# Moving the remaining additions of the values' products from VectorE to ScalarE and GpSimd, and building the identity matrix per stage

## The chip, the cores and the metric

The kernel runs on one NeuronCore of one Trainium2 chip. The metric is the device time of one execution in microseconds, the median of several. Besides TensorE (PE; its weight loads are listed as PEld) the core has VectorE (DVE), ScalarE (ACT), GpSimd (POOL) and SyncE (SP), which here issues all DMAs. Each engine works through its own instructions strictly in the order in which the program lists them and waits for the others through semaphores.

## The reference

The reference is a chain of four layers on `x` (8 sequences of 112 tokens, 512 channels) with a context `ctx` (8 x 375 rows, 512 channels), all in float32. Layer 0 is a cross attention. Layers 1 and 2 are recurrent blocks (RWKV): a time mix, whose core is a scan over the tokens, and a channel mix of three 512 x 512 products. Layer 3 is a decoder block with two cross attentions of 16 heads of 128 and an MLP.

```python
# layers 1 and 2, the scan over the tokens
a = k_l[..., :, None] * v_l[..., None, :]
out = jnp.einsum('bhs,bhst->bht', r_l, faaaa * a + s)
s_new = a + w_l[..., None] * s
# layer 3, in each of its two cross attentions
kh = (kv_in @ wk + bk).reshape(b, t, H, K)
vh = (kv_in @ wv + bv).reshape(b, t, H, K)
```

The values `vh` depend on the context and the weights alone, not on `x`. So they can be computed at any time before layer 3.

## The kernel before

**What fills what.** While layers 1 and 2 run, a generator `values()` computes the values of both attentions of layer 3, and two groups of keys, as a filler for TensorE. `fill(n)` takes its next n pieces. Its work is cut into 51 units; a unit multiplies a 2 x 2 arrangement of blocks by Strassen's scheme in Winograd's form, with seven products in place of eight, and the results are combined by additions. A product is two float32 matmuls 128x128x512, which the profile lists as four MATMUL records of L839.

**Banks.** The products of a unit go to two PSUM banks (tags `mm0` and `mm1`), and they alternate strictly: k1 in the first, k5 of the unit before in the second, then k6, k9 (of the unit before), k7, k2, k8, and the next unit has the banks exchanged. Each product is read out right after it: k1, k6 and k7 by a copy on ACT into a tile of the tag `v` (L922), k8 by a copy on ACT (L939), k2 by a copy on ACT into a tile of the tag `k2` and an addition on POOL (L932 and L933), k5 and k9 by an addition on DVE that reads PSUM and SBUF (L864 and L868). Until a bank has been read out, the second product after it can't start.

```python
p = bank(u, f, f"k5_{u}")
product(p, block(at), s["k5"])
nc.vector.tensor_add(u3, p, u3)
store(u3, u, 1, 1)
```

Every result is then written to memory by a DMA on SP (`store`, L855, L856 and L859), from where layer 3 reads it. SP also loads the context's blocks for the filler (`cv`, L823) and the rows of the values for the scan (`vj`, L534).

**The scan stages.** The function `time_mix` handles the recurrence in 64 steps (4 groups of channels times 16). There the order on PE, DVE, ACT and POOL is that of the source (`tc.manual_schedule(engines=ORDERED)`). A step has on DVE a product `kv` (L641, from PSUM and SBUF into PSUM) and the scan itself (L645, into `st`, two buffers); on ACT the copies of the next step's values into PSUM (`led`, L542 and L543), which wait for this step's `kv`, because `vp` has one buffer; on POOL the product `rs` (L649); on SP the load `vj` for three steps later (`spread`). Two fills stand in nearly every step: one between `kv` and `led`, the other after `rs`.

```python
nc.vector.tensor_mul(flat(kv), flat(vp), flat(k[:, c]))
fill(1)
vp = led(c * HS + at + 1)
...
nc.gpsimd.tensor_mul(by_batch(rs), st[:, :, :L], by_batch(r[:, c, :]))
waiting.append((c, j, rs))
fill(int(at not in (6, 10)))
```

After every fourth step TensorE sums `rs` (L622), and beside the steps run pieces of the group norm of the channels before (L561 to L583; its reciprocals on DVE, L575). Outside `manual_schedule` a scheduler places the instructions.

**The identity.** `ident`, 128 x 128, is made by two instructions of POOL at the start and stays in SBUF for the whole program. TensorE's transposes in layers 0 and 3 read it, and one subtraction (L743) at the start of the layers 1 and 2.

Of the kernel before, what the change touches and what calls it, by code (L numbers as in the profile page):

```python
# [22 lines left out]
F32 = mybir.dt.float32  # L23
# [6 lines left out]
P = 128  # L30
B, L, C, S = 8, 112, 512, 375
# [53 lines left out]
def halves(ap, h):  # L85

    return ap[..., h * NH : (h + 1) * NH]


def turned(ap):  # L90

    return ap.rearrange("p (h q r) -> p q h r", h=HB, q=4)


def turned_rows(ap, q):

    return ap.rearrange("(h q r) n -> q h r n", h=HB, q=4)[q]
# [11 lines left out]
def tile_kernel(ctx: ExitStack, tc: tile.TileContext, d: dict, out: bass.AP):  # L109
    nc = tc.nc  # L110

    const = ctx.enter_context(tc.tile_pool(name="const", bufs=1))
# [11 lines left out]
    def weight(name, g=None):  # L124

        w = wpool.tile([P, NC, C], F32, tag="w", name=f"w_{name}_{g}")
        nc.sync.dma_start(w, d[name] if g is None else d[name][g])
        return w

    x = xpool.tile([P, NC, N], F32, name="x")  # L130

    ident = const.tile([P, P], F32, name="ident")
    make_identity(nc, ident)
    mean_c = const.tile([P, P], F32, name="mean_c")
    nc.vector.memset(mean_c, 1.0 / C)
    eps = const.tile([P, 1], F32, name="eps")
# [12 lines left out]
    def mm(ps, name):  # L149
        return ps.tile([P, 512], F32, tag="mm", name=name)  # L150
# [65 lines left out]
    def layer0():  # L216
# [3 lines left out]
        with (  # L220
# [2 lines left out]
            tc.tile_pool(name="a0p", bufs=2, space=PSUM) as ps,  # L223
            tc.tile_pool(name="a0s", bufs=2, space=PSUM) as ps2,
        ):
            w_q, w_k = weight("L0_xattn_w_q"), weight("L0_xattn_w_k")
            nc.sync.dma_start(x, d["xT"])
            cxs = {}
# [69 lines left out]
            z = keep.tile([P, NC, N], F32, name="z0")  # L298
# [8 lines left out]
            for b in range(B):  # L307
# [7 lines left out]
                for t in range(3):  # L315
                    p = mm(ps, f"ps_r0_{b}_{t}")[:CT, :]
# [410 lines left out]
    def rwkv_layers():  # L727
        with tc.tile_pool(name="rc", bufs=1) as one:
            ones_t = one.tile([P, P], F32, name="ones_t")
            mean_h = one.tile([P, P], F32, name="mean_h")  # L730
            less_mean_h = one.tile([P, P], F32, name="less_mean_h")
            center_h = less_mean_h, mean_h
            pick = one.tile([P, 4, 4 * HB], F32, name="pick")
            with tc.tile_pool(name="rs", bufs=1) as setup:
                heads = setup.tile([P, P + P + HS - 1], F32, name="heads")
                nc.sync.dma_start(heads, d["heads"])

                nc.vector.tensor_copy(ones_t.rearrange("p (q h r) -> p q h r", q=4, h=HB), turned(heads[:, :P]))
                same = setup.tile([P, P], F32, name="same")
                for q in range(4):  # L740
                    nc.sync.dma_start(same[32 * q : 32 * (q + 1)], turned_rows(d["heads"][:, :P], q))
                nc.scalar.mul(mean_h.rearrange("p (q h r) -> p q h r", q=4, h=HB), turned(same), 1.0 / HS)
                nc.vector.tensor_sub(less_mean_h, ident, mean_h)  # L743

                for r in range(4):
                    at = P + HS - 1 - 4 * r
                    nc.vector.tensor_copy(pick[:, r], heads[:, at : at + 16 * HB - 3 : 4])
            first = one.tile([P, 2, NC, B], F32, name="first")
            nc.sync.dma_start(first, d["first"])
            for n in (1, 2):  # L750
                rwkv(n, ones_t, center_h, pick, first)


    def values():
# [8 lines left out]
        pool, spill, ps = shared["pool"], shared["spill"], shared["ps"]  # L763
# [4 lines left out]
        def tile_of(name):  # L768
            return pool.tile([P, C], F32, tag="v", name=name, bufs=6)
# [55 lines left out]
        def block(at):  # L825
            m = at // 2
            if m + 4 not in tiles:
                load(m + 4)
            return [tiles[m][:, n : n + P] for n in (at % 2 * BLOCK, at % 2 * BLOCK + CT)]
# [11 lines left out]
        def shaped(y, f):  # L841
            return y if f == "wv" else y[:, : HG * CT].rearrange("p (o s) -> p o s", o=HG)

        def bank(u, f, name):
            return shaped(ps.tile([P, C], F32, tag=f"mm{u % 2}", name=f"ps_v{name}"), f)

        def store(y, u, o, j):
# [10 lines left out]
            else:  # L858
                nc.sync.dma_start(where[:, t], y)  # L859

        def last_two(u, f, u2, u3, s, at):
            p = bank(u, f, f"k5_{u}")
            product(p, block(at), s["k5"])
            nc.vector.tensor_add(u3, p, u3)  # L864
            store(u3, u, 1, 1)
            yield "k5"
            product(p, block(at + 2), s["k9"], start=False)
            nc.vector.tensor_add(u2, p, u2)  # L868
            store(u2, u, 0, 1)
            yield "k9"  # L870

# [25 lines left out]
        for u, (at, unit) in enumerate(units):  # L897
            f, i, groups = sets[at]
            if unit == 0 and at == 2:

                for _ in before:
                    yield
                s = weights(at)
                yield
            elif unit == 0 and at:
                s = new
            if unit == UNITS - 2 and at != 1:
                new = {}
                steps = relay(at + 1, s, new)
                ready = next(steps)  # L910
            elif unit == UNITS - 1 and at != 1:
                following = ready
            if unit % 3 == 0:
                for gr in groups:
                    for b in (2 * (unit // 3), 2 * (unit // 3) + 1):
                        size = [P, 3, C] if f == "wv" else [P, 3, HG, CT]
                        shared[f, i, gr, b] = spill.tile(size, F32, name=f"{f}s{i}_{gr}_{b}")
            first, base, kept = bank(u, f, f"k1_{u}"), u * BLOCKS, []
            for what, n in (("k1", 0), ("k6", 2), ("k7", 4)):
                product(first, block(base + n), s[what], start=not n)  # L920
                kept.append(shaped(tile_of(f"{what}_{u}"), f))
                nc.scalar.copy(kept[-1], first)  # L922
                after(what)
                yield
                if n < 4:
                    yield from late()
            p1, u2, u3 = kept
            p = bank(u + 1, f, f"k2_{u}")
            product(p, block(base + 5), s["k2"])

            y = shaped(pool.tile([P, C], F32, tag="k2", name=f"k2_{u}"), f)
            nc.scalar.copy(y, p)  # L932
            nc.gpsimd.tensor_add(p1, y, p1)  # L933
            store(p1, u, 0, 0)
            after("k2")
            yield
            product(first, block(base + 6), s["k8"], start=False)
            y = shaped(tile_of(f"k8_{u}"), f)
            nc.scalar.copy(y, first)  # L939
            store(y, u, 1, 0)  # L940
            after("k8")
            yield
            before = last_two(u, f, u2, u3, s, base + BLOCKS + 1)
        for _ in before:
            yield
# [101 lines left out]

        return put

    def attention(i, h_in, work, kv, ps, ps2, keep, mlp_norm):  # L1050
        nonlocal filler
        pre = "L3_xattn_"
        scale = 1.0 / math.sqrt(HD)
# [64 lines left out]
        p = mm(ps, f"ps_bv{i}")[:, :HEADS]  # L1118
# [23 lines left out]
        for gr in range(NG):  # L1142
# [6 lines left out]
            for b in range(B):  # L1149
                u = f"{i}_{gr}_{b}"  # L1150
# [56 lines left out]
            if not ends:  # L1207
                add = add_to_x(None if gr else f"{pre}bo{i}")
# [63 lines left out]
    def layer3():  # L1272
        with (
            tc.tile_pool(name="t3v", bufs=2) as shared["pool"],
            tc.tile_pool(name="t3k", bufs=2) as kv,
            tc.tile_pool(name="t3", bufs=1) as keep,
            tc.tile_pool(name="t3w", bufs=2) as work,
            tc.tile_pool(name="t3p", bufs=2, space=PSUM) as ps,
        ):
            h_in = keep.tile([P, NC, N], F32, name="h_in")  # L1280
            with tc.tile_pool(name="t3s", bufs=1, space=PSUM) as ps2:
                def mlp_norm(h, bank):
                    if not h:
                        room = keep.tile([P, 3, 2, NH], F32, tag="t_h", name="t_mlp")
                        shared["t_mlp"] = room
                        squares = halves(h_in, 1)
                    else:
                        squares = halves(keep.tile([P, NC, N], F32, tag="q", name="room_mlp"), 1)
                    pre = "L3_xattn_ln_mlp_"
                    room = [None, squares] if h else [squares, None]  # L1290
                    room = room, shared["t_mlp"]
                    layer_norm_half(
                        ps, work, halves(h_in, h), h, pre + "scale", pre + "offset", "ln_mlp", room, bank
                    )

                for i in (1, 2):
                    attention(i, h_in, work, kv, ps, ps2, keep, mlp_norm)
            mlp(h_in, work, ps, keep, shared["t_mlp"])

    shared["spill"] = ctx.enter_context(tc.tile_pool(name="spill", bufs=1, space=bass.MemoryType.DRAM))  # L1300
# [84 lines left out]
```

## Time and profile before

| | |
|---|---|
| median of 3 runs | 3063.15 us (3061.47 to 3063.49) |
| profiled execution, its own time | 3068.96 us |
| span of its instructions | 3067.1 us |
| PE busy in the span | 2936.8 us (96%) |
| DVE, ACT, POOL busy in the span | 1698.1, 834.5, 767.3 us |
| first and second scan stage | 399 to 661 us, 1074 to 1345 us after the span's start |

The profile is of one execution. A row of a group of instructions gives its source line, engine, operation, output and inputs, sizes and count, then busy time, the mean of one, and the idle time of the engine just before it with what ended it. A row of waits gives who waited for whom: total, times, longest. The end of a matmul is modelled, so a short wait of PE can be hidden inside a busy time.

### The profile page before, as it was taken

How to read it: one execution, taken by the hardware profiler on the slowest of the kernel's cores; microseconds unless marked ns; L12 is line 12 of the kernel's file. 1: busy time of each engine (PE TensorE's matmuls, PEld its weight loads, DVE VectorE, ACT ScalarE, POOL GpSimd, SP SyncE). 2: the span in 40 equal slices, each digit the busy share in tenths (PEclk: the TensorE clock that was granted, in tenths of full speed). 3: DMA queues.
4: the chain of work that ended last, by engine and by line, in shares of the span. 5: the costliest groups of instructions: out<-in, count | busy, mean ns of one | idle time of the engine just before them, and what ended most of it. 6: DMA issues, size and time to landing. Idle time of an engine off the chain costs nothing.

```text
span 3067.1 us, 29702 instructions
## 1 busy us (share of the span) xinstructions
PE 2936.8 (96%) x10130; PEld 1585.1 (52%) x10130; DVE 1698.1 (55%) x2556; ACT 834.5 (27%) x1730; POOL 767.3 (25%) x668
## 2 busy tenths in 40 slices
PE   8989999998999999989989999999999999999999
PEld 4734433333434433337446666656566665656544
DVE  1433279876133289865165555655756454645555
ACT  2122145442232144532132222212222121212311
POOL 2232246642232257542210202020001101010030
PEclk9989999999999999999989999999999999999999
DMA  7322288963112299854234353424333343423110
GB/s 253 131 76 71 74 237 250 272 185 110 66 54 70 79 267 266 259 151 146 71 99 147 112 158 102 151 84 142 108 100 115 119 146 100 146 92 101 48 55 24
DMA packets 192054, 401.59 MB, mean 131 GB/s; under 512 B 26856, under 2 KB 112392, under 8 KB 185120
## 3 DMA queue, kind: packets, MB, share of 16 engines
q1 hardware_dynamic: 191904, 399.70, 42.0%
q8 instruction: 81, 1.33, 0.2%
q14 instruction: 69, 0.57, 0.1%
HBM read 321.85 MB, written 77.91 MB: 130 GB/s over the span
## 4 chain that ended last, share of the span: by engine, by line
PE 49%; DVE 2%; ACT 1%; issue 0%; POOL 0%; ACTq 0%; DVEq 0%; POOLq 0%
PE av L1180 6%; PE sc L1167 5%; PE ps_k1k L983 5%; PE ps_k7k L983 5%; PE ps_k5k L983 5%; PE pt L1170 3%; PE ps_k6k L983 2%; PE ps_k7q L983 2%; PE ps_k5q L983 2%; PE ps_k1q L983 1%; PE ps_k5o L983 1%; PE ps_k7o L983 1%; PE ps_k5fc L983 1%; PE ps_k7fc L983 1%; PE ps_k1o L983 1%; PE ps_k6q L983 1%
## 5 line engine op out<-in xcount | busy, mean ns | idle before, releaser
L839 PE MATMUL ps_vk<-wv,cv 128*128 128x512 f32 x1336 | 619.2, 611 | 52.4 <-DVE k L864 15.6
L839 PEld LDWEIGHTS ps_vk<-wv,cv 128*128 128x128 f32 x1336 | 251.5, 194 | 401.1 <-issue 303.0
L210 ACT ACTIVATE prob<-sc,top 112x376 f32<-112x376 f32 (+1 forms) x264 | 151.8, 575 | 709.6 <-DVE top L207 588.3
L649 POOL TENSOR_TENSOR rs<-st,r 128x896 f32<-128x896 f32 x128 | 246.7, 1928 | 226.7 <-DVE st L645 189.9
L645 DVE TENSOR_TENSOR_SCAN st<-decay,kv 128x904 f32<-128x904 f32 x128 | 260.4, 2035 | 15.6 <-DMA cv<-blocks 3.4
L1167 PE MATMUL sc<-k,q 128*112 128x376 f32 x512 | 200.6, 484 | 1.0 <-ACT prob L210 0.8
L1180 PEld LDWEIGHTS av<-pts,v 125*128 125x128 f32 (+1 forms) x1536 | 183.2, 191 | 30.0 <-DVE pts L1176 15.1
L1180 PE MATMUL av<-pts,v 125*128 125x112 f32 (+1 forms) x1536 | 186.6, 275 | 1.0 <-DVE pts L1176 1.0
L1160 POOL COPY k<-over_k 128x4 f32<-128x4 f32 x64 | 15.8, 253 | 678.3 <-PE sc L1167 610.0
L983 PE MATMUL ps_k1k<-cx,w_L_xattn_wk 128*128 128x375 f32 x480 | 177.1, 481 | 2.3 <-ACT rstdk L1001 2.3
L207 DVE TENSOR_REDUCE top<-sc 112x1 f32<-112x376 f32 (+1 forms) x264 | 143.6, 545 | 29.3 <-PE sc L1167 14.7
L641 DVE TENSOR_TENSOR kv<-vp,k 128x904 f32<-128x904 f32 x128 | 140.9, 1101 | 32.0 <-ACT vp L543 26.1
L922 ACT COPY k<-ps_vk 128x512 f32<-128x512 f32 (+1 forms) x153 | 89.0, 582 | 170.8 <-PE ps_vk L839 161.3
L1170 PEld LDWEIGHTS pt<-ident,prob 112*125 112x125 f32 (+1 forms) x768 | 97.6, 175 | 61.5 <-DVE prob L212 36.0
L212 DVE TENSOR_SCALAR prob<-prob,total 112x376 f32<-112x376 f32 (+1 forms) x264 | 120.7, 460 | 7.1
L983 PEld LDWEIGHTS ps_k1k<-cx,w_L_xattn_wk 128*128 128x128 f32 x480 | 89.3, 191 | 60.1 <-issue 3.2
L1170 PE MATMUL pt<-ident,prob 112*125 112x112 f32 (+1 forms) x768 | 116.3, 273 | 2.9 <-DVE prob L212 2.8
L543 ACT COPY vp<-vj 128x896 f32<-128x896 f32 x124 | 112.8, 910 | 11.6 <-DMA vj<-rows 7.6
L1187 DVE TENSOR_TENSOR ctxt<-av,bv 128x448 f32<-128x448 f32 x64 | 40.0, 624 | 126.6 <-PE av L1180 126.6
L933 POOL TENSOR_TENSOR k<-k,k 128x512 f32<-128x512 f32 (+1 forms) x51 | 67.4, 1322 | 133.6 <-ACT k L932 110.2
L1167 PEld LDWEIGHTS sc<-k,q 128*112 128x112 f32 x512 | 78.8, 176 | 41.1 <-ACT prob L210 6.1
L983 PE MATMUL ps_k7k<-cs,wsk 128*128 128x375 f32 x240 | 88.5, 480 | 0.6 <-DVE k L1088 0.6
(372 smaller groups left out, 4719.6 us busy)
## 6 DMA issues: line engine op xcount, KB each, us to landing
vj<-rows SPq DMA_DIRECT2D x124, 448.0 KB
cv<-blocks SPq DMA_DIRECT2D x181, 251.5 KB
cs<-blocks SPq DMA_DIRECT2D x120, 375.0 KB
wvs<-k SPq DMA_DIRECT2D x128, 256.0 KB
v<-wvs SPq DMA_DIRECT2D x64, 512.0 KB
cx<-in_ctxT SPq DMA_DIRECT2D x38, 750.0 KB
v<-wvs SPq DMA_DIRECT2D x64, 252.0 KB
wvs<-k SPq DMA_DIRECT2D x64, 224.0 KB
```

Of the source, the lines that this page charges most:

```text
L207: nc.vector.tensor_reduce(top, scores, AX.X, ALU.max, negate=True)
L210: nc.scalar.activation(prob, scores, AF.Exp, bias=top, accum_out=total)
L212: nc.vector.tensor_scalar(prob, prob, total, None, ALU.mult)
L543: nc.scalar.copy(vp[:, :, 1:], by_batch(vjs.pop((c, j))))
L641: nc.vector.tensor_mul(flat(kv), flat(vp), flat(k[:, c]))
L645: nc.vector.tensor_tensor_scan(flat(st), flat(decay[:, c]), flat(kv), 0.0, ALU.mult, ALU.add)
L649: nc.gpsimd.tensor_mul(by_batch(rs), st[:, :, :L], by_batch(r[:, c, :]))
L839: nc.tensor.matmul(to, left, right, start=start and n == 0, stop=k == 1, skip_group_check=True)
L983: nc.tensor.matmul(to, lhsT, rhs, start=start and k == 0, stop=k == 1, skip_group_check=not start)
L1167: nc.tensor.matmul(sc, q[:, o, tok], kt[:, o, :], start=True, stop=True)
L1170: nc.tensor.transpose(pt[t][:nt, o, :], prob[:, t0 : t0 + nt], ident[:L, :L])
L1180: nc.tensor.matmul(av[:, o, :], v[:nt, t, o * HD : (o + 1) * HD], pts[:nt, t, o, :], start=t == 0, stop=t == 2,)
```

## The change

k5 and k9 are read out as k2 was: a copy by ACT into a tile of the tag `k2`, and an addition by POOL. The tag `k2` gets two buffers. The identity is no longer kept throughout: it is made again in the pools of layer 0, of the setup of layers 1 and 2, and of layer 3.

```diff
-    ident = const.tile([P, P], F32, name="ident")
-    make_identity(nc, ident)
+    def identity(pool, name):
+        ident = pool.tile([P, P], F32, name=f"ident_{name}")
+        make_identity(nc, ident)
+        return ident
...
+            ident = identity(keep, "a0")
...
-                nc.vector.tensor_sub(less_mean_h, ident, mean_h)
+                nc.vector.tensor_sub(less_mean_h, identity(setup, "rs"), mean_h)
...
+        def add(y, p, u, f, what):
+
+            z = shaped(pool.tile([P, C], F32, tag="k2", name=f"{what}_{u}", bufs=2), f)
+            nc.scalar.copy(z, p)
+            nc.gpsimd.tensor_add(y, z, y)
+
         def last_two(u, f, u2, u3, s, at):
             p = bank(u, f, f"k5_{u}")
             product(p, block(at), s["k5"])
-            nc.vector.tensor_add(u3, p, u3)
+            add(u3, p, u, f, "k5")
             store(u3, u, 1, 1)
             yield "k5"
             product(p, block(at + 2), s["k9"], start=False)
-            nc.vector.tensor_add(u2, p, u2)
+            add(u2, p, u, f, "k9")
             store(u2, u, 0, 1)
             yield "k9"
...
-
-            y = shaped(pool.tile([P, C], F32, tag="k2", name=f"k2_{u}"), f)
-            nc.scalar.copy(y, p)
-            nc.gpsimd.tensor_add(p1, y, p1)
+            add(p1, p, u, f, "k2")
             store(p1, u, 0, 0)
...
-    def attention(i, h_in, work, kv, ps, ps2, keep, mlp_norm):
+    def attention(i, ident, h_in, work, kv, ps, ps2, keep, mlp_norm):
...
+            ident = identity(keep, "l3")
```

## The prediction

> **What bounds the kernel now.** I start with the busy shares of the page. PE is at 9 in almost every slice, so time is won only where PE stands still.
>
> ```profile
> span 3067.1 us, 29702 instructions
> PE   8989999998999999989989999999999999999999
> DVE  1433279876133289865165555655756454645555
> ```
>
> DVE's 7 to 9 in slices 6 to 9 and 15 to 18 mark the two scan stages. The table by windows gives the sums for the first (399 to 661), the stretch between, and the second (1074 to 1345); the columns are length, PE, PEld, DVE, ACT, POOL.
>
> ```profile
> 399.00:661.00 262.00, 246.36 (x729) 98.74 (x730) 235.44 (x175) 126.49 (x235) 162.37 (x96) 0.97 0.86 254
> 661.00:1074.00 413.00, 394.99 (x951) 175.19 (x950) 146.50 (x164) 103.69 (x187) 113.62 (x125) 0.96 0.26 81
> 1074.00:1345.00 271.00, 252.60 (x747) 101.46 (x746) 235.80 (x177) 129.46 (x238) 163.37 (x97) 0.98 0.87 252
> ```
>
> PE and DVE are both near full there (94% and 90%), and in-order queues tie them together. Next, PE's waits over the whole program:
>
> ```profile
> PE ps_vk L839 <- DVE k L864: 15.6, 10, 5.8
> PE ps_vk L839 <- DVE k L868: 14.0, 9, 3.1
> ...
> PE ps_vk L839 <- ACT k L922: 6.8, 7, 2.4
> PE ps_vk L839 <- ACT k L939: 6.1, 5, 1.7
> ```
>
> The two longest are the additions that the change moves: 29.6 us in 19 waits, 9.8 in the first stage, 12.8 in the second, 7.0 elsewhere. The timeline shows one:
>
> ```profile
> 506.37 1.53 DVE L575 RECIPROCAL gsq<-gsq 128x224 f32<-128x224 f32 x1
> ...
> 507.82 1.08 DVE L641 TENSOR_TENSOR kv<-vp,k 128x904 f32<-128x904 f32 x1
> 508.81 0.68 DVE L864 TENSOR_TENSOR k<-ps_vk,k 128x512 f32<-128x512 f32 x1
> ...
> 509.54 1.13 PE L839 MATMUL ps_vk<-wv,cv 128*128 128x512 f32 x2 [2.22 <-DVE k L864]
> ```
>
> PE's product was done near 507.3; its addition stood in DVE's queue behind a reciprocal and the `kv` after it, and PE waited 2.22 us for the bank.
>
> **What the Trainium skill says.** "PSUM — Partial Sum Buffer" (The four PSUM rules): GpSimd can't touch PSUM; hence the copy by ACT. The trace agrees in so far as no POOL row reads a PSUM tile. "Perfetto Trace Analysis" (Matmuls): groups should rotate through banks so that one's evacuation overlaps the next one's matmuls. Here two banks alternate; the 2.22 us are that overlap failing. "SBUF — State Buffer" (Who interferes with whom): a DVE instruction with two SBUF inputs contends with GpSimd instructions that read SBUF. The trace agrees: in the scan stages, where `vp` and `kv` lie in PSUM, L933 takes 1260 to 1291 ns; beside L691 (two SBUF inputs) it took 2.51 and 2.37 us, and L691 itself 671 to 2759 ns.
>
> **The change part by part.**
>
> *DVE loses 102 additions* (2 for each of 51 units, median 0.68 us), 17 units in each stage: 34 x 0.68 = 23 us, to 212 us. What PE gets depends on where the fill stands. Ahead of the step's `led`, the copy by ACT needs only the product: in the first stage three waits (2.2, 1.4, 2.7) vanish, 6.4 us. After the scan, the DVE addition ended 2.03 + 0.68 = 2.71 us after `kv`; on ACT it stands behind `led`, 0.17 + 0.91 + 0.58 = 1.66 us after `kv`, so at most 1.05 us of each is gained. Capping the nine waits of this kind at 1.05 each, 6.7 us go; the two at a stage's first steps (2.2 and 3.1), where `led` is done long before, go whole, 5.3. Together 18.4 of 22.6. Of the 7.0 us elsewhere I take 6.5: the largest, 5.8 us at 760, is an addition behind DVE's L691 while ACT is idle. **Gain 25 us** (bounds 15 and 29.6).
>
> *ACT gets 102 copies* of 0.585 us: 34 x 0.585 = 20 us per stage, 146 of 262, not a bound. But its copies make PE wait too: 12.9 us for the 255 of L922, L932 and L939, 0.05 each; 102 more: **loss 5 us** (0 to 10). Queued behind them are `led`, and with it DVE's next `kv`.
>
> *POOL gets 102 additions* of 1.27 us (L933): 34 x 1.27 = 43 us per stage, 162 to 206. It fits the stage. Queued behind an addition, which now waits for ACT, is `rs`, and for `rs` wait the sums L622 (slack of two steps) and, by the two buffers of `st`, the scan two steps on: a slack of about 1.1 + 2.03 + 1.1 after a scan's end, less 1.93 of `rs`, 2.3 us. One addition fits; it doesn't where the relay of weights puts POOL additions of 2.6 us (L783's row) beside it, once per stage: **loss 2 us** (0 to 6). Outside the stages 34 additions can collide with DVE's two-input operations, each up to 1.2 us, mostly beside PE work: **loss 1 us** (0 to 8).
>
> *SP issues the same DMAs in the same number*, but the stores of k5 and k9 now wait for POOL. SP's waits in the first stage:
>
> ```profile
> SPq L859 <- POOL k L933: 38.2, 11, 5.3
> ...
> SPq L855 <- POOL k L933: 14.5, 5, 4.3
> SPq L859 <- DVE k L864: 9.7, 7, 2.7
> SPq L859 <- DVE k L868: 9.1, 8, 2.8
> SPq L855 <- DVE k L868: 8.1, 5, 1.8
> SPq L855 <- DVE k L864: 7.7, 5, 2.4
> ```
>
> A store behind POOL waits 52.7 / 16 = 3.3 us, one behind DVE 34.6 / 34 = 1.0. The 34 moved stores come 2.3 us later, and behind them stand `cv` loads (issued eight products ahead, so covered) and the next `vj`. From the DMA packets of the 124 `vj` loads I took when each had landed and when ACT's copy began: the slack has a median of 5.3 us, but 9 loads have under 1.2. The shortfall, the sum of (2.3 - slack) where positive, is 17 us; 34 of 64 steps have a moved store: 9 us. It delays ACT and DVE, which now have room, so I take about half: **loss 5 us** (0 to 19, the latter for a delay of 3.1).
>
> *The k2 buffers.* A copy waits for the addition two before it, four products or some 7 us earlier; nothing (up to 2 us of loss if POOL is late).
>
> *The identity*: two more pairs of a memset (0.20) and a select (0.29) on POOL. The one of the setup runs while POOL waits 57.9 us for weights (L780), and its reader L743 comes 20 us later; the one of layer 3 stands beside a wait of PE of 9.2 us (for the norm's mean), whose DVE sums run slow beside POOL's additions: between -1 and +1 us, I take 0. Freed and added SBUF move addresses; in the built program the loads at the filler's start wait for the same instructions as before: 0.
>
> Sum: 25 - 5 - 2 - 1 - 5 = **12 us faster**. On its own time the profiled execution would go from 3068.96 (span 3067.1 and 1.9 around it) to 3057. The median of the runs is 5.8 us below that execution, so the prediction is 3063.15 - 12 = **3051 us**.
>
> **The rivals.**
> 1. *The cover holds* and ACT's queue costs nothing: 25 to 29.6 us less POOL's 2, 3035 to 3040. For it: median slack of 5.3 us of `vj`, DVE 50 us below the stage. Against: ACT already makes PE wait 12.9 us.
> 2. *The wait only changes its owner*: ACT's copy stands behind `led`, which waits for `kv`, which waits for the reciprocal; PE waits as before. ACT gives a third of the gain or nothing: 25/3 less 8 is 0, so 3057 to 3067. For it: at 1257 PE waited 2.2 us for L864, and ACT's own copy then came only at 1258.79, after `led`. Against: in eleven of the 14 waits of the stages `led` was done before PE began to wait.
> 3. *Slower: SP's queue becomes the pacemaker.* Late stores make `vj` late, ACT waits with `led` and all copies behind it, PE for the banks. At 2.3 us of delay the unhalved price is 9 us, at 3.4 us it is 0.53 x 44 = 24, at 4.0 it is 0.53 x 65 = 35. It decides from about 3 us on, where it and the 8 of ACT and POOL eat the gain; at 4 us the time is 3063 - 25 + 8 + 35 = 3081. For it: POOL's additions stand behind a `rs` of 1.93 us, and single stores waited up to 5.3. Against: SP is often early (27.1 us of waits of `cv` loads for PE in the first stage), so part of the delay is idle time.
> 4. *POOL becomes the bound* by contended additions of 2.5 us: 162 - 17 x 1.27 + 51 x 2.5 = 268 us per stage, over the 262 of now, some 3080. It decides from 2.04 us each (245 us per stage). Against it: 1291 ns is the longest there. 2 in 100, counted with 3.
>
> That the change doesn't do what it says is excluded by the built program: DVE 102 fewer instructions, ACT 102 more, POOL 106 more, PE and SP as many as before and in nearly the same order.
>
> **How the numbers follow.** A measurement of this kernel can tell about 0.2%, 6 us, from no change. Forecast (3044 to 3057): 0.42. Rival 1: 0.25. Rival 2: 0.17. Rivals 3 and 4: 0.16. Faster is the first two, 0.67; same rival 2, 0.17; slower 0.16. The range goes from 3032, a little below rival 1 (0.07 left out), to 3069, where 0.13 of rival 3 is left out. The faster cases alone span 3032 to 3057.
>
> **What would show it.** Right: PE's waits for the bank of k5 and k9 name ACT and sum to under 12 us; both stages are shorter by 5 to 10 us each; L869's additions take 1.27 us in the stages; SP's waits for POOL grow to over 130 us per stage; waits of ACT's L543 copy for `vj` grow from 7.6 us by about 10. Wrong: these waits grow by over 30 us (rival 3), PE's waits for ACT reach 25 us (rival 2), or POOL's additions are much longer than 1.3 us in the stages (rival 4).

## The result and the profile after

| | before | after |
|---|---|---|
| median | 3063.49 us (5 runs, 3061.47 to 3071.53) | 3051.93 us (5 runs, 3042.98 to 3054.23) |
| ratio | | 0.994, 95% interval 0.9924 to 0.9956 |
| profiled execution | 3068.96 us | 3052.01 us |

By the medians of these runs the change makes the kernel 11.6 us (0.4%) faster, where 12 were forecast. The ratio, which is estimated from all runs, says 0.6%, 18 us (13 to 23); in a second series it was 0.9937 (0.9917 to 0.9957), 19 us. Compared at one clock of PE (explained below) the gain is 13.9 us. So the sum came out about right, but partly by luck: its gain was too small by 7 to 11 us and its price by 6 to 9, and these errors cancelled.

The page of the changed kernel, its head first and then three of its groups (busy time, mean of one, idle time before them and its cause):

```profile
span 3050.0 us, 29875 instructions
...
PE   8989999999999999999899999999899999999999
...
DVE  1533268866223287856265565655756564645555
...
L649 DVE TENSOR_TENSOR_SCAN st<-decay,kv 128x904 f32<-128x904 f32 x128 | 260.7, 2037 | 24.5 <-POOL rs L653 6.4
L869 POOL TENSOR_TENSOR k<-k,k 128x512 f32<-128x512 f32 (+1 forms) x153 | 201.1, 1315 | 239.3 <-ACT k L868 207.3
...
L547 ACT COPY vp<-vj 128x896 f32<-128x896 f32 x124 | 112.8, 910 | 22.7 <-DMA vj<-rows 18.9
```

Most lines have moved by a few; the copy is now L868 and the addition L869, for k2, k5 and k9 alike. DVE's scan (L649) has a new wait for POOL, 6.4 us, and ACT's copy of `vj` (L547) waits 18.9 us where in the kernel before it waited 7.6:

```profile
ACT vp L543 <- DMA vj<-rows: 7.6, 5, 2.5
```

The table by windows, for the first scan stage, the stretch between, and the second (length, then busy time of PE, PEld, DVE, ACT, POOL, then PE's clock):

```profile
405.00:661.00 256.00, 242.79 (x731) 98.74 (x732) 218.57 (x142) 145.14 (x269) 204.11 (x130) 0.99 0.89 260
661.00:1067.00 406.00, 392.08 (x946) 174.64 (x945) 142.97 (x147) 111.16 (x201) 138.54 (x141) 0.96 0.26 82
1067.00:1328.00 261.00, 249.01 (x749) 101.42 (x748) 218.73 (x142) 147.10 (x273) 205.45 (x131) 0.99 0.90 259
```

From its first `kv` to its last, the first stage is shorter by 6.9 us (263.1 to 256.2), the second by 11.1 (271.6 to 260.5), the stretch between by 5.7. Part of this is the clock. Intervals at half clock took 6.8 and 5.1 us of full clock from the two stages before, 3.4 and 1.7 here. In a second profile of the changed kernel (`a2_changed`), where they took 5.1 and 6.8, the stages are shorter by 5.4 and 5.6 us. POOL has 204 us of work in the first stage and is no bound. The stretch ahead of the first stage is 5.8 us longer here; the profiles below put that down to the clock for the most part.

PE's waits over the whole program (total, times, longest):

```profile
PE ps_vk L843 <- ACT k L932: 10.5, 9, 2.4
...
PE ps_vk L843 <- ACT k L868: 6.9, 5, 3.3
PE ps_gm L565 <- ACT gsq L566: 6.5, 6, 3.3
...
PE ps_vk L843 <- ACT k L946: 3.6, 3, 1.4
```

No bank waits for DVE any more. The four rows of before summed to 42.5 us; the three of now (L932, L868, L946) make 21.0.

### The profile page after: what moved, and what is told of

It reads as the page before. It is cut to its first block, busy times and chain, and to the rows that moved or that the text cites. A ratio compares the mean times of both kernels' runs of the same rounds, so it can differ in the third digit from the quotient of the medians.

```text
span 3050.0 us, 29875 instructions
## 1 busy us (share of the span) xinstructions
PE 2931.5 (96%) x10130; PEld 1585.6 (52%) x10130; DVE 1656.9 (54%) x2454; ACT 888.3 (29%) x1832; POOL 898.6 (29%) x774
## 4 chain that ended last, share of the span: by engine, by line
PE 82%; DVE 7%; POOL 4%; DMA 3%; issue 3%; ACT 2%; SPq 0%; DVEq 0%; POOLq 0%; ACTq 0%
PE ps_vk L843 12%; PE av L1187 6%; PE sc L1174 5%; PE ps_k1k L990 5%; PE ps_k7k L990 5%; PE ps_k5k L990 5%; PE ps_o L161 3%; PE pt L1177 3%; PE ps_k6k L990 2%; PE ps_r L472 2%; PE ps_k L472 2%; PE ps_v L472 2%; DVE st L649 2%; PE ps_k7q L990 2%; PE ps_fk L161 2%
## 5 line engine op out<-in xcount | busy, mean ns | idle before, releaser
L843 PE MATMUL ps_vk<-wv,cv 128*128 128x512 f32 x1336 | 606.4, 604 | 34.3 <-ACT k L932 10.5
L649 DVE TENSOR_TENSOR_SCAN st<-decay,kv 128x904 f32<-128x904 f32 x128 | 260.7, 2037 | 24.5 <-POOL rs L653 6.4
L869 POOL TENSOR_TENSOR k<-k,k 128x512 f32<-128x512 f32 (+1 forms) x153 | 201.1, 1315 | 239.3 <-ACT k L868 207.3
L1187 PEld LDWEIGHTS av<-pts,v 125*128 125x128 f32 (+1 forms) x1536 | 184.8, 193 | 29.7 <-DVE pts L1183 14.5
L1177 PEld LDWEIGHTS pt<-ident_l,prob 112*125 112x125 f32 (+1 forms) x768 | 97.4, 176 | 61.5 <-DVE prob L215 35.9
L868 ACT COPY k<-ps_vk 128x512 f32<-128x512 f32 (+1 forms) x153 | 89.1, 583 | 136.1 <-PE ps_vk L843 135.5
L932 ACT COPY k<-ps_vk 128x512 f32<-128x512 f32 (+1 forms) x153 | 89.0, 582 | 114.6 <-PE ps_vk L843 111.2
L547 ACT COPY vp<-vj 128x896 f32<-128x896 f32 x124 | 112.8, 910 | 22.7 <-DMA vj<-rows 18.9
L1177 PE MATMUL pt<-ident_l,prob 112*125 112x112 f32 (+1 forms) x768 | 116.1, 273 | 2.7 <-DVE prob L215 2.6
```

What stands on the lines that cost most here:

```text
L649: nc.vector.tensor_tensor_scan(flat(st), flat(decay[:, c]), flat(kv), 0.0, ALU.mult, ALU.add)
L843: nc.tensor.matmul(to, left, right, start=start and n == 0, stop=k == 1, skip_group_check=True)
L869: nc.gpsimd.tensor_add(y, z, y)
L1177: nc.tensor.transpose(pt[t][:nt, o, :], prob[:, t0 : t0 + nt], ident[:L, :L])
L1187: nc.tensor.matmul(av[:, o, :], v[:nt, t, o * HD : (o + 1) * HD], pts[:nt, t, o, :], start=t == 0, stop=t == 2,)
```

## The experiments

**How they are compared.** Runs of one kernel differ by up to 24 us, and they follow the mean clock that was granted to PE: a common slope fitted within the kernels through 143 timed runs is -2.05 us for each 0.001 of clock, and it leaves about 2 us of scatter (3.3 and 4.5 us for the runs of `e1_identity` and `e6_vj5`). So beside each measured ratio stands the mean time brought to a clock of 0.981; two such means differ reliably from some 3 us on, for `e6_vj5` from 4. Whether a kernel causes its clock isn't settled by this, so both columns are given. The rows come from three series, each with its own runs of the kernel before (medians 3064.0, 3070.0, 3066.7; at one clock 3063.8, 3064.9, 3063.1). The second holds `e4_k2_one`, `e5_st3`, `e6_vj5` and `e9_no_add_outside`, and no run of the changed kernel. Measured from the kernel before in their own series, these four would look 1.2 us better than below.

| run | median us | ratio to before (95%) | mean clock | us at 0.981 |
|---|---|---|---|---|
| before, all series | 3065.8 | 1 | 0.9801 | 3063.7 |
| changed, first runs | 3051.9 | 0.9940 (0.9924 to 0.9956) | 0.9816 | 3050.3 |
| `e1_identity` | 3063.4 | 0.9999 (0.9984 to 1.0013) | 0.9804 | 3062.5 |
| `e2_dve_copy` | 3078.2 | 1.0038 (1.0023 to 1.0054) | 0.9811 | 3077.3 |
| `e3_no_add` | 3023.8 | 0.9870 (0.9851 to 0.9889) | 0.9852 | 3033.0 |
| `e7_late_store` | 3043.9 | 0.9939 (0.9922 to 0.9955) | 0.9837 | 3050.7 |
| `e4_k2_one` | 3051.6 | 0.9938 (0.9918 to 0.9957) | 0.9823 | 3053.6 |
| `e5_st3` | 3043.7 | 0.9912 (0.9889 to 0.9935) | 0.9842 | 3049.3 |
| `e6_vj5` | 3039.9 | 0.9899 (0.9878 to 0.9920) | 0.9852 | 3047.5 |
| `e9_no_add_outside` | 3042.2 | 0.9906 (0.9885 to 0.9927) | 0.9834 | 3045.9 |
| `a2_changed` | 3045.3 | 0.9937 (0.9917 to 0.9957) | 0.9833 | 3049.4 |
| `e10_st3_vj4` | 3043.0 | 0.9933 (0.9914 to 0.9952) | 0.9825 | 3046.3 |
| `e11_all` | 3056.0 | 0.9972 (0.9961 to 0.9984) | 0.9798 | 3054.3 |
| `e12_no_add_inside` | 3035.1 | 0.9904 (0.9883 to 0.9924) | 0.9848 | 3042.0 |

At one clock the changed kernel (11 runs of two series, 3049.8) is 13.9 us faster than before.

### The identity alone (`e1_identity`)

Against the kernel before, `ident` is built by stages as in the diff, and k5 and k9 stay with DVE:

```diff
         def last_two(u, f, u2, u3, s, at):
...
-            add(u3, p, u, f, "k5")
+            nc.vector.tensor_add(u3, p, u3)
...
-            add(u2, p, u, f, "k9")
+            nc.vector.tensor_add(u2, p, u2)
```

(The minus lines are those of the changed kernel; `k2` has one buffer.)

> The identity by stages alone; k5 and k9 are still added by DVE. Forecast's term: 0, so 3063 us, ratio to the kernel before 1.000 (0.998 to 1.002). Rival: the 5.8 us by which the first scan stage of the changed kernel starts later (404.9 against 399.1 us) come from the identity or from moved addresses; then the stage starts at about 405 us here too, and the time is near 3069 us, ratio 1.002.

The ratio is 0.9999, so the identity and the moved addresses cost nothing that can be told. PE's waits (L874 and L878 are the additions by DVE here) are those of before:

```profile
PE ps_vk L843 <- DVE k L874: 16.3, 13, 5.8
PE ps_vk L843 <- DVE k L878: 14.6, 8, 3.1
```

The first stage began at 402.1 us in this profile, at 399.1 in that of before, and in the changed kernel at 404.9 in one profile and at 392.3 in the other. The clock's records explain most of this spread: in the changed kernel's two profiles the half-clock intervals ahead of the stage took away 25.6 and 10.2 us of full clock. One and the same kernel starts the stage 12.6 us apart, so the later start is not shown to be an effect of the edit.

### DVE copies, POOL adds (`e2_dve_copy`)

```diff
-            nc.scalar.copy(z, p)
+            (nc.scalar.copy if what == "k2" else nc.vector.tensor_copy)(z, p)
```

> As the changed kernel, but DVE copies k5 and k9 out of PSUM instead of ACT, so that DVE keeps as many instructions as before and only POOL's additions and SP's later stores are new. Forecast's sum: no gain of 25, no 5 of ACT, but the losses of POOL (2 + 1) and SP (5): 8 us slower than the kernel before, 3071 us, ratio 1.0026. Rival (POOL and SP cost nothing, all of the change is what PE waits for): 3063 us, ratio 1.000. Rival (SP's queue is the pacemaker): over 3080 us, ratio over 1.005.

The copy takes DVE 68.9 us in 102 times, as the additions of before did (69.0), so this run has all that the change adds on POOL and SP and nothing of what it takes from DVE. PE's waits (L868 is the copy of k5 and k9):

```profile
PE ps_vk L843 <- DVE k L868: 29.2, 19, 2.8
...
PE ps_vk L843 <- ACT k L932: 6.9, 7, 2.4
PE ps_vk L843 <- ACT k L946: 6.0, 5, 1.7
```

29.2 us in 19 waits is what before had (29.6 in 19). The run is 13.6 us slower than before at one clock (ratio 1.0038): this is the price of the new additions and stores while DVE copies, where 8 were forecast. And it is 27.5 us slower than the changed kernel, which differs from it in nothing but the engine of the copy: the move to ACT, its own stalls taken off, is worth 27.5 us, where the forecast had 25 - 5 = 20. The price need not be made of the same parts in both kernels: POOL's additions make DVE's operations 3.4 us longer in sum here (1774.7 us against 1771.3 before), 16.3 in the changed kernel (1718.6 against 1771.3 - 69.0). The rival with SP's queue as pacemaker (over 3080) falls.

### Without POOL's additions (`e3_no_add`)

```diff
         def add(y, p, u, f, what):
 
+            if what != "k2":
+                nc.scalar.copy(y, p)
+                return
             z = shaped(pool.tile([P, C], F32, tag="k2", name=f"{what}_{u}", bufs=2), f)
```

> As the changed kernel, but ACT's copy of k5 and k9 goes straight into the tile that is stored, and POOL's addition is left out (two of the four blocks of each value lack a term). DVE is as free as in the changed kernel, POOL as busy as before, and the stores wait for ACT alone. Forecast's sum: gain 25 less 5 of ACT, without the 8 of POOL and SP: 3043 us, ratio 0.9935. Rival (these losses are nothing): as the changed kernel, 3051 us, ratio 0.996. Rival (they are more than double): under 3035 us, ratio under 0.991.

The ratio of 0.987 is that of the rival: 16.8 us less than the changed kernel at one clock, so the new additions and what follows from them cost about twice the forecast's 8. The run also gives the gain without any price of POOL and SP: it is 30.7 us faster than the kernel before at one clock, where the forecast had 20.

### Where this price lies: outside and inside the stages (`e9_no_add_outside`, `e12_no_add_inside`)

A flag is set around the 64 steps of each scan stage. The first run leaves the additions of k5 and k9 out where it isn't set (17 units), the second, with `shared.get("scan")` without the `not`, where it is (34 units):

```diff
-            z = shaped(pool.tile([P, C], F32, tag="k2", name=f"{what}_{u}", bufs=2), f)
+            if what != "k2" and not shared.get("scan"):
+                nc.scalar.copy(y, p)
+                return
+            z = shaped(pool.tile([P, C], F32, tag="k2", name=f"{what}_{u}", bufs=2), f)
```

> As the changed kernel, but POOL's addition of k5 and k9 is left out in the 17 units outside the scan stages (there ACT copies into the tile that is stored; some blocks of the values lack a term). Theory (contention outside: in the changed kernel DVE's L694 group takes 131.4 us against 120.1 where all these additions are left out, and the partial sums of the norms 51.9 against 46.1): this alone gives about 10 us of the 17, 3040 us at the same clock, ratio near 0.992. Forecast's term (1 us): 3049 us, ratio 0.995. Rival (the cost lies in the stages): as the changed kernel, 3050 us.

Outside, it is 3.9 us at one clock, four times the forecast's 1, but not 10. (The 131.4 and 120.1 us of the expectation are sums over the operations of that kind in layers 1 and 2; the line named there, L695 here, has 44.3 and 34.0.) Here is what POOL's additions do to DVE's operations with two SBUF inputs. First the changed kernel's groups on DVE by line (busy time, mean ns), then the same in this run, where L695 has become L697:

```profile
L695 DVE SCALAR_TENSOR_TENSOR xk<-sxc,vecs,xc 128x448 f32<-128x448 f32 x16 | 25.5, 1642 | 6.6 <-POOL sxc L355 6.2
...
L179 DVE TENSOR_TENSOR part_mean_ln<-part_mean_ln,x 128x448 f32<-128x448 f32 x16 | 18.2, 1136 | 0.4
```

```profile
L697 DVE SCALAR_TENSOR_TENSOR xk<-sxc,vecs,xc 128x448 f32<-128x448 f32 x16 | 21.5, 1392 | 6.2 <-POOL sxc L355 5.7
...
L179 DVE TENSOR_TENSOR part_mean_ln<-part_mean_ln,x 128x448 f32<-128x448 f32 x16 | 14.4, 898 | 0.4
```

One `xk` takes 1642 ns on the mean in the changed kernel, where additions of k5 and k9 fall beside some of them, and 1392 without these additions (1367 in the kernel before). Over all of DVE this is 17.9 us of longer operations (1718.6 against 1700.7 us, summed over instructions). PE's waits show what comes through. The longest of them, first in the changed kernel, then in this run:

```profile
PE ps_t L422 <- DVE xx L412: 11.0, 14, 3.5
```

```profile
PE ps_t L422 <- DVE xx L412: 9.0, 12, 3.5
```

With `xk` (4.4 and 3.9) and the norms' partial sums (3.8 and 1.6), PE waits 19.2 us for such operations in the changed kernel and 14.5 here: 4.7 us less, near the 3.9. The rest of the 17.9 lies beside PE's work. That such operations get longer is what "SBUF — State Buffer" (Who interferes with whom) of the Trainium skill lets one expect, and the trace agrees.

> As the changed kernel, but POOL's addition of k5 and k9 is left out in the 34 units inside the scan stages (some blocks of the values lack a term); the complement of the run that left it out outside. If the two parts add up to the 17 us at the same clock of the run that left out all: 13 us faster than the changed kernel beside it. Forecast's terms for the stages (POOL 2, SP 5): 7 us faster. Rival (the cost of POOL and SP in the stages lies beside PE's work): under 3 us faster.

Inside, it is 7.8 us (10 us by the medians of the two kernels in this series), near the 7 that the forecast's POOL and SP terms made. But what these 7 consisted of was wrong, as the waits of ACT show in this run:

```profile
ACT vp L547 <- DMA vj<-rows: 17.0, 11, 3.3
ACT v L583 <- POOL v L581: 14.7, 16, 2.6
```

No store waits for these additions here, and ACT still waits 17.0 us for `vj` (20.4 in the changed kernel of the same series). What falls, beside the scan's wait for `rs` (6.4 to 0.9 us), is another wait: that of ACT's last step of the group norm (L583, before L579) for POOL's multiplication ahead of it (L581, before L577). In the changed kernel and in the kernel before it is

```profile
ACT v L583 <- POOL v L581: 22.1, 16, 4.8
```

```profile
ACT v L579 <- POOL v L577: 14.6, 13, 2.6
```

The multiplication stands behind POOL's new additions, and behind ACT's waiting instruction stand the copies that free the banks. That wait was in no term of the forecast. How many of the 7.8 us it carries was not tried alone.

PE's own waits show where the price inside arrives. PE's sums (L626) wait for `rs` 4.5 us in the changed kernel of the same series and 2.0 here:

```profile
PE ps_y L626 <- POOL rs L653: 4.5, 3, 2.2
```

```profile
PE ps_y L626 <- POOL rs L654: 2.0, 2, 1.0
```

For the group norm's square on ACT, PE waits 6.1 us there and 4.5 here, for ACT's releases of the banks 23.1 and 20.3. Together that is 33.7 against 26.8, 6.9 us (5.1 with the first profile of the changed kernel).

The two parts make 11.7 us, both together 16.8: with an uncertainty of 2 us or more, some 4 to 5 us remain unexplained.

### The terms inside the stages (`e7_late_store`, `e5_st3`, `e6_vj5`, `e10_st3_vj4`)

The store of k5 goes one piece later:

```diff
             add(u3, p, u, f, "k5")
-            store(u3, u, 1, 1)
             yield "k5"
             product(p, block(at + 2), s["k9"], start=False)
+            store(u3, u, 1, 1)
```

> As the changed kernel, but the store of k5 is issued one piece later, behind the product of k9, where POOL has added by then; in SP's queue a load of the filler and the next vj now come ahead of it. Forecast's term of SP (5 us, of which k5 has about half): SP's waits for POOL in the first stage fall from 107 to about 60 us, ACT's waits for vj from 18.9 to about 12 us, and the time by 2 to 3 us to 3049, ratio 0.995. Rival (late vj costs nothing, since kv of DVE waits beside PE's work): waits fall, the time stays at the changed kernel's.

SP's waits for POOL in the first stage, which in the changed kernel are

```profile
SPq L863 <- POOL k L869: 68.8, 33, 5.2
SPq L859 <- POOL k L869: 38.2, 15, 4.9
```

fell only to 100 us (62.9 + 37.2, over 396 to 657), those of ACT for `vj` in both stages not at all (18.9 and 18.8), and at one clock the time is that of the changed kernel (+0.9 us). The edit moved less than was meant, so it is a weak test of SP's term.

A third buffer for `st`, in the tile of the first two `vj` (`early`), which is free after the second step:

```diff
-                        st = work.tile([P, B, LP], F32, tag="st", name=f"st{n}_{c}_{j}", bufs=2)
+                        if (c * HS + at) % 3 == 2:
+                            st = early[:, : B * LP].rearrange("p (b l) -> p b l", b=B)
+                        else:
+                            st = work.tile([P, B, LP], F32, tag="st", name=f"st{n}_{c}_{j}", bufs=2)
```

> As the changed kernel, with three buffers of st (the third lies in the unused part of the tile that holds the first vj). DVE's waits of the scan for rs, 6.3 us in 3 times, should go. Forecast's term of POOL: 2 us, so 3048 us. Theory after the first runs (POOL and SP cost 13 to 17 us at the same clock, most of it contention of POOL's additions with DVE outside the scan stages): at most 4 us faster than the changed kernel, ratio 0.994 to 0.995. Rival (most of the cost comes through st in the stages): 8 us or more faster, ratio under 0.993.

The scan's waits for `rs`, 6.4 us, are gone, and at one clock the time falls by 0.5 us, which can't be told from 0, nor from the forecast's 2.

Five buffers for `vj`, loaded four steps ahead:

```diff
-                    if at < 2:
-                        vjs[c, j] = early[:, at * N : (at + 1) * N]
+                    if at % 5 < 2:
+                        vjs[c, j] = early[:, at % 5 * N : (at % 5 + 1) * N]
...
-            for at in range(3):
+            for at in range(4):
...
-                        spread(c * HS + at + 3)
+                        spread(c * HS + at + 4)
```

> As the changed kernel, with five buffers of vj in place of three (the tile that holds the first two is used on), each loaded four steps ahead instead of three. ACT's waits for vj, 18.9 us in both stages, should fall under 5 us. Forecast's term of SP: 5 us faster than the changed kernel, ratio 0.993. Theory after the first runs (the wait for vj fell only from 18.9 to 12.7 us where no store waited for POOL's addition, so late stores aren't its main cause, and little of it reaches PE): 0 to 2 us, ratio near 0.995. Rival of the prediction (SP's queue is what costs): over 8 us, ratio under 0.992.

ACT's waits for `vj` fell from 18.9 to 2.7 us:

```profile
ACT vp L547 <- DMA vj<-rows: 2.7, 2, 2.6
```

and at one clock the time fell by 2.3 us, with a scatter of 4.5, so this run alone doesn't exclude the forecast's 5. The scan's waits for `rs` grew from 6.4 to 9.7 us here. The ratio, 0.9899, looks better, but this kernel also had a high clock, 0.9852, in a series where the kernel before had its lowest.

> As the changed kernel, with three buffers of st and four of vj, each vj loaded four steps ahead. Theory (in the stages PE is busy 95% of the time and these waits of DVE and ACT lie beside its work): 1 us of st and 3 of vj at the same clock, so about 4 us faster than the changed kernel beside it. Rival (each of the two waits hides the other's cost, and together they are the 8 us of POOL and SP in the stages): 8 us or more faster. Rival (nothing): as the changed kernel.

Both together (`early` holds one `st` and one `vj`) took both waits away and gave 3.5 us at one clock. Measured beside the changed kernel, the ratios to before, 0.9933 and 0.9937, can't be told apart. So late `vj` and late `rs` together cost 3 us or so of the 7.8 inside the stages.

### One buffer of `k2` (`e4_k2_one`)

```diff
-            z = shaped(pool.tile([P, C], F32, tag="k2", name=f"{what}_{u}", bufs=2), f)
+            z = shaped(pool.tile([P, C], F32, tag="k2", name=f"{what}_{u}", bufs=1), f)
```

> As the changed kernel, with one buffer of the tag k2 in place of two. A copy by ACT then waits for the addition of the product before. Products stand some 3.4 us apart in a run of fills (four matmul records of 0.43 us, two of them between a copy and the next), the copy and the addition take 0.58 + 1.27 us, and a rs of 1.93 us can stand between them: 3.8 us, so that about every second copy is late by some 0.4 us or more. If ACT's queue carries that to PE: 10 us slower than the changed kernel, 3060 us, ratio near 0.998. Rival (the second buffer does nothing): 3050 us, ratio 0.995.

The waits come as expected. The first row is ACT's copy, the second PE's wait for it:

```profile
ACT k L868 <- POOL k L869: 41.0, 23, 4.1
```

```profile
PE ps_vk L843 <- ACT k L868: 18.4, 18, 3.3
```

PE's waits for the banks of L868 grow from 6.9 to 18.4 us, but the time by only 3.8 us at one clock (2.6 if measured from before in its own series; the ratio, 0.9938, shows no difference), where 10 were expected.

### The change in the stages alone (`e11_all`)

As the run with three `st` and four `vj`, and outside the stages DVE adds again:

```diff
+            if what != "k2" and not shared.get("scan"):
+                nc.vector.tensor_add(y, p, y)
+                return
```

> As the run with three buffers of st and four of vj, but outside the scan stages k5 and k9 are added by DVE again, so that POOL's additions stand beside DVE's operations with two SBUF inputs no more than before. Forecast's terms: 6.5 us of waits of PE for DVE come back, 1 us of contention goes: 5 us slower than the run without this edit. Theory of contention (about 4 us outside): 2 us slower to equal. Rival (contention outside is 10 us): 3 us faster.

It is slower than the run without this edit by 8.0 us at one clock, by 13 in the medians of the same series. DVE's additions are back in PE's waits (L874 is that addition here):

```profile
PE ps_vk L849 <- DVE k L874: 10.2, 6, 5.8
```

So the 17 units outside the stages, to which the forecast gave 6.5 - 1 = 5.5 us before ACT's own stalls, bring about 8 us at one clock, contention paid.

At one clock none of the versions that keep all additions beats the changed kernel by more than can be told here.

## Why the prediction was right, point by point

| term of the sum | forecast, us | measured at one clock, us |
|---|---|---|
| DVE relieved, less ACT's own stalls | 25 - 5 = 20 | 27.5 (copy on ACT against copy on DVE) to 30.7 (additions left out, against before) |
| POOL, contention and SP together | -8 | -13.6 (DVE copying) to -16.8 (additions left out) |
| of these inside the stages (POOL 2, SP 5) | -7 | -7.8 |
| of these outside (contention 1) | -1 | -3.9 |
| identity | 0 | 1.2 faster, not told from 0 |
| sum | 12 | 13.9 (27.5 - 13.6 or 30.7 - 16.8) |

The forecast was right in what makes PE wait, in most of what the new work queues ahead of, and in that the gain exceeds the price. That 12 came so near 13.9 is luck: both the gain and the price were too small.

- **The bound and the waits** were read rightly. PE waits for bank releases, and of the 29.6 us for k5 and k9, 6.9 were left, below the 12 that were named as the mark; all of them name ACT (L868 holds k2's copies too). ACT's other copies make PE wait 14.1 us where it was 12.9. So 6.9 + 1.2 = 8.1 us of stalls stand where the forecast left 4.6 of the 29.6 and added 5, 9.6.
- **The gain of 25, less 5, was mis-sized**, though the named waits were not by much: the term counted only PE's named waits for the banks. These fell by 21.5 us in the changed kernel (42.5 to 21.0) and by 24 without the additions (to 18.7). Between the run with DVE's copies and the changed kernel they fell by 21.1 us (42.1 to 21.0), and PE's busy time by another 7.0 (2938.5 to 2931.5), both at a clock of 0.980. Together this is about the 27.5. That the 7 us are waits too short to be shown fits, as the end of a matmul is modelled, but no run shows it. And most of the 7 us needn't have been in the kernel before: its busy time, 2936.8 us at a clock of 0.978, would be about 2933 at 0.980 (an estimate from the two profiles of the changed kernel, 2931.5 us at 0.980 and 2924.2 at 0.983).
- **Where the excess lies** follows only from differences between runs, each with 2 to 3 us of uncertainty. Outside the stages the change brings 8 us and has paid 3.9 for them, 11.9, where the forecast had 6.5. Inside it brings 13.9 - 8 and has paid 7.8, 13.7, where the forecast had 18.4. Of ACT's 5 us a part belongs to each. This points outside the stages, and the cause there stays open.
- **Rival 1** had the higher gain, but no loss beside POOL's 2; its 3035 to 3040 is where the kernel would be if the additions cost little (`e3_no_add` 3033). **Rival 2** falls with the 6.9 us; all bank waits that name ACT are 21.0, under the 25 set as its mark. **Rival 4** falls: in the stages an addition took 1256 to 1299 ns.
- **SP's 5 us, and rival 3**: the observations were half right. ACT's waits for `vj` grew by 11, as said. SP's waits for POOL reached 107 and 108 us per stage, not 130, since a store waited 107 / 48 = 2.2 us and not 3.3. But the inference failed: where no store waits for these additions, `vj` is waited for 17 us all the same, and taking the waits for `vj` and `rs` away together gave 3.5, where the forecast had 5 + 2. The step "the shortfall delays ACT and DVE, about half" put a price on a wait that the late stores for the most part don't cause. What makes `vj` late instead stays open.
- **POOL's 2 us** for `rs` and `st`: the scan's waits came (6.4 us) and cost 0.5 to 1.7. PE's sums, to which the prediction gave a slack of two steps, wait for `rs` too, 4.4 us where it was 2.5, most of it at the end of each stage. Beside them came the wait of the group norm through POOL, 7.5 us longer, that the part on POOL's queue had not named: it followed `rs` and not the multiplication L577 that stands in the same queue.
- **Contention, 1 us**, was too low by about 3: the collisions make DVE's operations 17.9 us longer, and more of that came through to PE (4.7 us of waits) than the forecast's "mostly beside PE work" allowed.
- **The two stages** got shorter by 6.9 and 11.1 us in one profile and by 5.4 and 5.6 in the other, against 5 to 10 each. The k2 buffers' 0 holds with two of them; one would cost 3 to 4.

## What to carry to other kernels

Work that is moved to an idle engine costs what stands behind it in that engine's queue, so list all of that, not only the next instruction: here a multiplication of the group norm stood there too, with the bank copies behind its reader. Relief of the bounding engine was worth more here than the fall of its named waits (27.5 us for 21.1, 30.7 for 24), and a wait of another engine mostly less (16 us of waits for `vj` were worth 2 to 4). Where errors of several us can cancel, test the gain and the price each by its own run, such as the same copy on the old engine, and compare at one clock.

## What the runs showed of the hardware

The profile's clock falls to half speed in intervals of 3.4 us or two or three times that: 133.7 us of them in the profile of before, 123.7 and 102.9 in the two of the changed kernel, 86.2 without the additions inside. From run to run the time follows the clock by as much as the change brings (a clock of 0.975 to 0.984 in the runs of before, 18 us on the common slope). "TensorE: Matmul & The Clock Gate" (What's actually happening) in the Trainium skill describes a free-running window of about 3.4 us whose idleness halves the clock. The length agrees. In the profile of before, 15 of the 28 intervals follow 1.9 to 3.4 us of idle PE within the 7 us ahead of them, mostly less than a whole window (as at 406 us in the first stage, and at 1082 and 1314 in the second). Others don't: at 887.5, 904.6 and 921.7 us, 17.1 us apart, the records show no idle PE in the 7 us before. The kernels with more relief of PE tend to have the higher clock (0.9801 before, 0.9848 and 0.9852 in the two runs without additions in the stages), but so has `e6_vj5` (0.9852). Whether fewer stalls cause this stays open, and with it which of the two columns above is nearer to what the change is worth.

The additions on POOL and DVE's operations with two inputs in SBUF are longer where they meet. `xk` took 1642 ns on the mean with the additions and 1392 without. An addition took at most 1.3 us in the stages, where `vp` and `kv` lie in PSUM, and up to 3.0 us elsewhere.
